# Softmax sums of two attention layers: pairs on VectorE, accumulating DMAs for the rest

## The chip, the cores and the metric

The kernel runs on one core of one Trainium2 chip. The metric is the device time of one execution in microseconds (us), lower is better. The three timed runs of the kernel before lie between 2926.52 and 2927.66 us, with a median of 2927.6 us.

## The reference, cut to what matters

The input is x of shape (4, 64, 64, 64): four images, each of 4096 tokens with 64 channels, all float32. Four attention layers follow each other. The change touches only layers 2 and 3, which have the same core once queries, keys and values are there:

```
# layer 2, per image (layer 3: the same with h for xn and other weights; it returns h + proj)
w   = jnp.einsum('bchw,bcHW->bhwHW', q, k) * scale     # 4096 x 4096 scores
w   = jax.nn.softmax(w.reshape(B, H, W, H * W), axis=-1)
out = jnp.einsum('bhwHW,bcHW->bchw', w, v)
out = linear_last(out, Wp, bp)
return out + residual
```

The softmax needs, for each of 4096 queries, the sum of 4096 exponentials. The kernel takes no maximum first; it computes exp(score) directly, multiplies it with the values, and divides by the sum at the end.

## The kernel before, in words

**Tiles.** An image lies in SBUF as [128, 2048]: 64 channels of one half of the tokens on partitions 0 to 63, of the other half on 64 to 127. `attention` (layers 2 and 3, from line 1272) walks over 4 chunks c of 1024 queries, and within a chunk over 32 blocks j of 128 keys. `first(u)` (u = 32 c + j) makes the scores of one key block on TensorE, four matmuls of 64x64 tiles into a PSUM tile `s` of 128 keys x 1024 queries (line 1288), and ScalarE turns them into a tile `p` of exponentials (line 1293). Only two `s` tiles exist, and `p` tiles come from a pool of 14 buffers. `then(u)` (line 1323) multiplies `p` with the values and accumulates in PSUM.

**Sums.** VectorE adds the 32 `p` tiles of a chunk into one tile `zacc`, element by element: 31 additions of 128x1024 (line 1299). The sum over the 128 keys of a block is left to `turn_blocks`: a transpose by blocks of 32 (line 1307), a reduction over 32 columns (`sum_blocks`, line 1311, giving `zsums`), and eight small matmuls on TensorE that add the rest (`sums`, line 1242). Then VectorE takes the reciprocal, and `turn` (line 1257) transposes and divides the output `o`.

**Order.** The schedule is written out by hand: the order of calls is the order of instructions on each engine. One `step` makes two key blocks: `first(2t)`, `first(2t+1)`, then the two `then` of two steps ago with a piece of background work between them (`advance(MID)`) and after or in the middle of the second (`advance(LATE)`), and last whatever was put on the list `later`. `before[n]` runs at the start of step n. `urgent` holds work with a due step. Background work is the preparation of other images and layer 1 of another image, one piece per `yield`. With t the last step of a chunk, the order before is: `turn_blocks` at the end of step t, `sum_blocks` at the end of step t+1, the last `then` of the chunk in step t+2 followed on ScalarE by a copy of half the output (line 1332) and on VectorE by adding the other half (line 1333), and `turn` with its `sums` matmuls in the middle of step t+4 (line 1334 puts it on `urgent`). There are 4 chunks x 2 layers x 4 images = 32 chunks. The very last one of the kernel is handled by `final` instead of `turn`.

**Queues.** Instructions of an engine start in order. SP issues nearly all DMAs. GpSimd (POOL) runs in this part only the power function in `inverse_root` (line 767), for the normalisations, and at the very end two stores.

## Time and profile before

| | us |
|---|---|
| median of the timed runs | 2927.6 |
| span of the profiled execution (first to last instruction; its time is not given apart from it) | 2927.0 |
| TensorE matmuls busy | 2895.3 (99%) |
| VectorE busy | 1871.5 (64%) |
| of it `zacc` additions of line 1299, 960 + 32 | 1174.2 + 38.9 |
| ScalarE busy | 1800.3 (62%) |
| GpSimd busy | 35.2 (1%) |
| DMA engines, mean busy share of queue q1 | 4.8% |

Busy time is the time in which an engine worked on at least one instruction. A busy TensorE need not run at its peak, since matmuls overlap, so the pace of a step is read from start to start. The mean granted clock of TensorE is 0.998 of full speed. In the profile's groups a row has the line, engine, operation, names and shapes, the count, the busy time, the mean of one in ns, and the idle time of the engine before it with what ended it.

### The profile page before, as it was taken

The page shows a single profiled execution, that of the slowest core. Times are in us where ns is not written, and L with a number is a line of the kernel's source. Part 1 is how long each engine was busy: PE and PEld are TensorE (multiplying, and loading weights), DVE is VectorE, ACT ScalarE, POOL GpSimd, SP SyncE. Part 2 cuts the span into 40 slices and gives each one's busy share as a digit, 9 for nine tenths or more (in the row PEclk, how much of TensorE's full clock was granted, in tenths as well). Part 3 has the DMA queues.
Part 4 walks back from the last instruction along what each step waited for, and adds up shares of the span by engine and source line. Part 5 has one row for each costly group of instructions (what it writes and reads, how often), then busy time and mean ns, then how long its engine had stood idle before and what let it go on. Part 6 is the DMA issues. An engine that isn't in the chain of part 4 may idle for free.

```text
span 2927.0 us, 66546 instructions
## 1 busy us (share of the span) xinstructions
PE 2895.3 (99%) x29397; PEld 1113.6 (38%) x29397; DVE 1871.5 (64%) x2141; ACT 1800.3 (62%) x2481; POOL 35.2 (1%) x35
## 2 busy tenths in 40 slices
PE   9999999999999999999999999999999999999998
PEld 3333233333444433344443343333344444443333
DVE  2111753589821078963027897888888877878878
ACT  5666666665566766566766655555555655555554
POOL 0000000000000000000000000000000000000000
PEclk9999999999999999999999999999999999999999
DMA  2010000000001000000000000000000000000000
GB/s 38 1 30 7 1 1 16 7 5 5 19 5 30 1 7 5 5 23 16 1 1 7 5 9 19 19 5 9 5 19 8 20 5 8 6 20 5 8 5 10
DMA packets 85513, 30.64 MB, mean 10 GB/s; under 512 B 79168, under 2 KB 83264, under 8 KB 83808
## 3 DMA queue, kind: packets, MB, share of 16 engines
q1 hardware_dynamic: 83168, 25.87, 4.8%
q8 instruction: 232, 3.80, 0.6%
q10 hardware_dynamic: 1984, 0.38, 0.1%
q14 instruction: 65, 0.53, 0.1%
q0 software_dynamic: 64, 0.07, 0.0%
HBM read 4.79 MB, written 4.19 MB: 3 GB/s over the span
## 4 chain that ended last, share of the span: by engine, by line
PE 97%; DVE 1%; ACT 1%; issue 0%; DMA 0%; POOL 0%; ACTq 0%; DVEq 0%
PE acc L1323 30%; PE s L1288 30%; PE s L999 15%; PE acc L1028 15%; PE s L1122 2%; PE acc L1148 2%; ACT p L1128 1%; DVE zacc L1299 1%; PE s L1148 1%; PE s L891 0%; PE s L912 0%; PE s L1419 0%; PE s L1467 0%; PE s L1092 0%; PE s L1194 0%
## 5 line engine op out<-in xcount | busy, mean ns | idle before, releaser
L1293 ACT ACTIVATE p<-s 128x1024 f32<-128x1024 f32 x1024 | 994.6, 1022 | 696.2 <-PE s L1288 676.5
L1299 DVE TENSOR_TENSOR zacc<-zacc,p 128x1024 f32<-128x1024 f32 x960 | 1174.2, 1223 | 179.7 <-ACT p L1293 114.8
L1323 PE MATMUL acc<-p,v 64*64 64x512 f32 (+1 forms) x8576 | 1006.6, 573 | 0.0
L1009 ACT ACTIVATE p<-s 128x1024 f32<-128x1024 f32 x480 | 487.3, 1020 | 114.8 <-PE s L999 114.6
L1323 PEld LDWEIGHTS acc<-p,v 64*64 64x64 f32 x8576 | 340.4, 133 | 545.1 <-issue 545.1
L1028 PE MATMUL acc<-p,vs 64*64 64x512 f32 (+1 forms) x4224 | 501.4, 577 | 0.0
L1288 PE MATMUL s<-q,k 64*64 64x512 f32 x2048 | 491.6, 590 | 2.1 <-ACT p L1128 2.1
L999 PE MATMUL s<-xT,q 64*64 64x512 f32 x2048 | 487.2, 591 | 2.4 <-DVE mean L1355 0.7
L1288 PE MATMUL s<-q,xT 64*64 64x512 f32 x2048 | 489.5, 591 | 0.0
L999 PE MATMUL s<-xT,q_swapped 64*64 64x512 f32 x2048 | 487.6, 591 | 0.3 <-DVE o L1157 0.3
L1288 PE MATMUL s<-q,h_swapped 64*64 64x512 f32 x2048 | 481.0, 591 | 3.9 <-DVE v L916 3.5
L1288 PE MATMUL s<-q,k_swapped 64*64 64x512 f32 x2048 | 480.4, 590 | 0.0
L1011 DVE TENSOR_REDUCE all_z<-z 128x1 f32<-128x4 f32 x128 | 20.1, 157 | 606.5 <-ACT p L1009 606.2
L1028 PEld LDWEIGHTS acc<-p,vs 64*64 64x64 f32 x4224 | 173.3, 133 | 266.0 <-issue 264.2
L1288 PEld LDWEIGHTS s<-q,h_swapped 64*64 64x64 f32 x2048 | 145.5, 133 | 144.5 <-issue 131.7
L1288 PEld LDWEIGHTS s<-q,k_swapped 64*64 64x64 f32 x2048 | 148.1, 133 | 137.6 <-issue 87.2
L999 PEld LDWEIGHTS s<-xT,q_swapped 64*64 64x64 f32 x2048 | 146.2, 133 | 141.8 <-issue 110.3
L1288 PEld LDWEIGHTS s<-q,xT 64*64 64x64 f32 x2048 | 145.7, 133 | 138.1 <-issue 131.7
L999 PEld LDWEIGHTS s<-xT,q 64*64 64x64 f32 x2048 | 144.2, 133 | 139.3 <-issue 110.8
L1288 PEld LDWEIGHTS s<-q,k 64*64 64x64 f32 x2048 | 148.6, 133 | 116.7 <-issue 96.2
L1017 ACT ACTIVATE vs<-v,all_r 128x64 f32<-128x64 f32 x256 | 89.1, 348 | 157.2 <-PE acc L1028 80.3
L1128 ACT ACTIVATE p<-s 128x1024 f32<-128x1024 f32 x128 | 124.1, 1022 | 82.4 <-PE s L1122 78.5
(213 smaller groups left out, 1319.6 us busy)
## 6 DMA issues: line engine op xcount, KB each, us to landing
k_swapped<-k SPq DMA_DIRECT2D x8, 512.0 KB, 5.8
residual<-turned SPq DMA_DIRECT2D x128, 32.0 KB, 1.9
h_swapped<-xT SPq DMA_DIRECT2D x8, 512.0 KB, 5.3
out_dram<-turned SPq DMA_DIRECT2D x60, 64.0 KB, 2.0
xin<-in_x_dram SPq DMA_DIRECT2D x12, 256.0 KB, 6.8
q_swapped<-q SPq DMA_DIRECT2D x6, 512.0 KB, 5.5
pg<-pg SPq DMA_DIRECT2D x8, 128.0 KB, 2.3
xin<-in_x_dram SPq DMA_DIRECT2D x12, 64.0 KB, 2.4
```

The lines of the kernel that those rows point to most:

```text
L999: nc.tensor.matmul(s[half(e), chunk(i)], queries(m, i, e), k[half(i), chunk(c)], start=True, stop=True)
L1009: nc.scalar.activation(p, s, AF.Exp, accum_out=z)
L1011: nc.vector.tensor_reduce(zsum[:, m : m + 1], zs.pop(m), AX.X, ALU.add)
L1017: nc.scalar.activation(vs, v[:, m, :], AF.Copy, scale=rz[:, m : m + 1])
L1028: nc.tensor.matmul(acc[c][half(i), cols], scaled[t][half(e), :], ps[NC * m + c][half(e), chunk(i)][:, cols], start=(m == 0 and not second) ...
L1122: nc.tensor.matmul(ss[e][half(m), chunk(i)], pgs[0 if e == d else 1][r, ds(n * P + m * C, C)], th[r, chunk(i ^ j)], start=True, stop=True,)
L1128: nc.scalar.activation(pk[e], ss[e], AF.Exp)
L1148: nc.tensor.matmul(acc[quarter(q), :], g[:, k, :], ps[j, k][q // 2][:, chunk(q % 2)], start=(k == 0 or not bank), stop=(k == NK - 1 or not ...
L1288: nc.tensor.matmul(s[half(e), chunk(i)], k[(j + i) % 2][half(i), ds(j // 2 * P + e * C, C)], q[half(i), chunk(c)], start=True, stop=True,)
L1293: nc.scalar.activation(p, s, AF.Exp)
L1299: add = lambda: nc.vector.tensor_tensor(zaccs[c], p0, p, ALU.add)
L1323: nc.tensor.matmul(accs[c][e][half(i), cols], v[half(e), j, :], p[half(e), chunk(i)][:, cols], start=(j == 0), stop=(j == NB - 1),)
```

## The change

VectorE no longer adds every `p` to `zacc`. In every step it adds the two new key blocks to each other. The first two pairs of a chunk (n = 0 and 1) are the two accumulators of the chunk; they lie in a pool of three `zacc` buffers instead of two. Each later pair (n = 2 to 15) goes to a tile of the `p` pool, and a DMA issued by GpSimd adds it into accumulator n % 2. The `p` pool has 13 buffers instead of 14. `turn_blocks` runs two steps later than before and first adds the two accumulators. In the last chunk of the kernel (`at_once`) VectorE adds the pairs itself and `turn_blocks` keeps its place.

```diff
-    x_p, p_p, z_p, o_p = pool("x", 13), pool("p", 14), pool("z", 2), pool("o", 2)
+    x_p, p_p, z_p, o_p = pool("x", 13), pool("p", 13), pool("z", 2), pool("o", 2)
@@ attention, first(u)
             p = ps[u] = p_tile()
             nc.scalar.activation(p, s, AF.Exp)
-            if j == 1:
-                zaccs[c] = z_p.tile([P, 1024], FP, tag="zacc", name="zacc")
-            if j >= 1:
-
-                p0 = ps[u - 1] if j == 1 else zaccs[c]
-                add = lambda: nc.vector.tensor_tensor(zaccs[c], p0, p, ALU.add)
-                later.append(add) if j % 2 or urgent_now() or ready(MID) else add()
+            if j % 2:
+                p0, n = ps[u - 1], j // 2
+                at_once = c == NC - 1 and final is not None
+                pair = p_tile() if n > 1 else z_p.tile([P, 1024], FP, tag="zacc", name="zacc", bufs=3)
+                if n < 2:
+                    zaccs[c, n] = pair
+
+                def add():
+                    nc.vector.tensor_tensor(pair, p0, p, ALU.add)
+                    if n > 1 and at_once:
+                        nc.vector.tensor_tensor(zaccs[c, n % 2], zaccs[c, n % 2], pair, ALU.add)
+                    elif n > 1:
+                        nc.gpsimd.dma_start(zaccs[c, n % 2], pair, accum_op=ALU.add)
+
+                later.append(add)
             if j == NB - 1:
-                later.append(lambda: turn_blocks(c))
+                if at_once:
+                    later.append(lambda: turn_blocks(c))
+                else:
+                    before.setdefault(now[0] + 2, []).append(lambda: later.append(lambda: turn_blocks(c)))
 
         def turn_blocks(c):
 
             t = p_tile()
-            nc.vector.transpose(t, zaccs.pop(c))
+            z = zaccs.pop((c, 0))
+            nc.vector.tensor_tensor(z, z, zaccs.pop((c, 1)), ALU.add)
+            nc.vector.transpose(t, z)
 
             def sum_blocks():
                 zsums[c] = small.tile([P, 32], FP, tag="zsums", name="zsums")
```

## The prediction

> **What bounds the kernel now.** I read the busy rows and slices, then the costliest groups, then short windows, then what VectorE does around the places that the change moves.

> ```profile
> span 2927.0 us, 66546 instructions
> PE 2895.3 (99%) x29397; PEld 1113.6 (38%) x29397; DVE 1871.5 (64%) x2141; ACT 1800.3 (62%) x2481; POOL 35.2 (1%) x35
> DVE  2111753589821078963027897888888877878878
> L1299 DVE TENSOR_TENSOR zacc<-zacc,p 128x1024 f32<-128x1024 f32 x960 | 1174.2, 1223 | 179.7 <-ACT p L1293 114.8
> ```

> TensorE is busy for all but 31.7 us. The next view is one step of two key blocks in layer 3 without background work (columns: stretch, length, then busy time and count of PE, PEld, DVE, ACT and POOL, granted clock, DMA share, GB/s):

> ```profile
> 2012.50:2015.93 3.43, 3.43 (x36) 1.20 (x32) 2.45 (x2) 1.94 (x2) 0.00 (x0) 1.00 0.02 5
> ```

> A step lasts 3.43 us at full clock, PE covers all of it, and VectorE needs 2.45, so in a plain step VectorE hides. Of the steps without background work, nearly all last 3.43; one in layers 2 and 3 stands out with 9.8 us, at 1784.8:

> ```profile
> 1783.26 1.23 DVE L916 TENSOR_TENSOR v<-s,bv 128x1024 f32<-128x1024 f32 x1 [3.33 <-PE s L912]
> 1784.40 2.54 DVE L1299 TENSOR_TENSOR zacc<-zacc,p 128x1024 f32<-128x1024 f32 x2
> 1786.98 1.25 DVE L1307 STREAM_TRANSPOSE p<-zacc 128x1024 f32<-128x1024 f32 x1
> 1788.15 1.19 DVE L916 TENSOR_TENSOR v<-s,bv 128x1024 f32<-128x1024 f32 x1
> 1789.39 1.12 PE L1288 MATMUL s<-q,h_swapped 64*64 64x512 f32 x2 [3.53 <-DVE v L916]
> ```

> There PE waits 3.53 us for a second L916 that stands behind two `zacc` additions and the transpose, and the windows show the clock at 0.50 from 1789.4 to 1795.3. Elsewhere VectorE is off the path. So the ceiling of a gain is small, and what matters is what becomes late.

> **The change part by part.** The programs as built have the same order of instructions on PE, ACT and SP; only VectorE and POOL differ.

> *Fewer additions.* 992 of 1.22 us become 512 pairs, 14 more in the last chunk, and 32 that join the two accumulators: 558, or 434 x 1.22 = 530 us less on VectorE. Hidden under PE in plain steps: 0. At 1784.8 only one pair (1.22) stands before the second L916 instead of 2.54 + 1.25, so it ends near 1786.75 and PE restarts near 1786.8 instead of 1789.39: 2.6 us. The idle gap is then about 1 us, for which I expect no clock loss, and half of 5.9 us, 2.95, comes back too. Gain 5.5 us; without the clock's part 2.6.

> *The later turn.* This is the part on the path. The view is a chunk boundary in layer 3, VectorE's rows, then one row of PE:

> ```profile
> 2017.33 1.25 DVE L1307 STREAM_TRANSPOSE p<-zacc 128x1024 f32<-128x1024 f32 x1
> 2018.61 1.22 DVE L1311 TENSOR_REDUCE zsums<-p 128x32 f32<-128x1024 f32 x1
> 2023.63 0.69 DVE L1333 TENSOR_TENSOR o<-o,acc 128x512 f32<-128x512 f32 x1 [1.55 <-ACT o L1332]
> 2024.24 5.14 DVE L1299 TENSOR_TENSOR zacc<-zacc,p 128x1024 f32<-128x1024 f32 x4
> ...
> 2028.81 0.25 PE L1242 MATMUL s<-zsums,lanes 64*64 64x16 f32 x8
> ```

> `zsums` is ready at 2019.83, 9 us before PE wants it. In the new order on VectorE the addition of the accumulators and the transpose stand behind L1333 (end 2024.32), then comes pair n = 1 of the next chunk, then the reduction. From the end of L1333: addition 1.22, transpose 1.25, pair 1.22, reduction 1.21, with the small gaps and overlaps of neighbours here 4.79, and 0.15 until PE starts (reduction end to matmul at the kernel's end: 2916.72 to 2916.87): 4.94 us. Before, 4.49 us lie between the end of L1333 and the matmul. PE is in order, so the second `then` and all that follows wait 0.45 us. PE is the bound, so it is lost.

> There are 31 such boundaries (the last chunk keeps its place). Asking the timeline at each for the end of L1333 and the start of L1242 gives 4.37 to 4.49 us at 23, 6.27 at 3, 5.14 at 2, 3.67 at 2, 5.48 at one. The built order shows what else stands before the reduction. 23 x 0.47 = 10.7. Of these, three (second chunk of layer 2 beside layer 1) have two operations of L1187/L1188 there, 0.68 + 0.71 each: +4.2; three have one in-place scaling of h (0.81, 0.81, 0.74): +2.3; one a tiny reduction: +0.2. The 6.27 ones have two layer-1 additions: 4.94 + 2.45 - 6.27 = 1.1 each, 3.4. The 5.14 ones: 0. The 3.67 ones have a tiny reduction (0.22) in place of the pair: 0.3 each, 0.5. The 5.48 one has two of L1424: 0.8. Sum 22.1 us.

> *The end.* In the last chunk the chain after the last exponential (2912.45) is pair, add to accumulator, join, transpose, reduce instead of the rest of two additions, transpose, reduce:

> ```profile
> 2911.56 2.55 DVE L1299 TENSOR_TENSOR zacc<-zacc,p 128x1024 f32<-128x1024 f32 x2 [0.88 <-ACT p L1293]
> 2914.22 1.25 DVE L1307 STREAM_TRANSPOSE p<-zacc 128x1024 f32<-128x1024 f32 x1
> ```

> Three additions from 2912.45 end near 2916.2 instead of 2914.11. PE already waits for `zsums` there: +1.9 us.

> *The DMAs.* 434 of 512 KB, one per 3.43 us. Before has none, so I bound one. Nearest rows:

> ```profile
> k_swapped<-k SPq DMA_DIRECT2D x8, 512.0 KB, 5.8
> residual<-turned SPq DMA_DIRECT2D x128, 32.0 KB, 1.9
> out_dram<-turned POOLq DMA_DIRECT2D x2, 32.0 KB, 3.0
> ```

> They may take long in two ways. The built program makes DMA n wait on POOL for DMA n-2 (same accumulator), so each must land within 2 x 3.43 = 6.87 us of its issue; and the join waits for DMA 15, issued about 4.5 us after the start of step t, while VectorE reaches the join 11.8 us after it: 7.3 us. `k_swapped` goes as two transfers, issued 0.5 us apart: 1 MB in about 6.3 us; less 1.9 fixed that is 2.2 us per 512 KB. [...] Below 0 there is nothing: no DMA replaces one on the path.

> *Buffers.* 13 `p` buffers also hold pairs. In the built program most pair buffers are written again three or four steps later (10 us or more), but 36, beside layer 1, are taken by an exponential two steps later. Steps there last 5.64 us, so 2 x 5.64 + 2.1 - 4.5 = 8.9 us for the DMA: 0 at 5.4 us. Past that ACT stalls, and with two `s` tiles PE follows.

> *POOL's own work.* `pow` for the normalisations (5.4 us at 128x32, 1.5 at 128x1) now shares its queue with waiting DMA issues. Of the layer-2 ones only one falls among the DMAs; it holds DMA issues by 5.4 us once, and the joins come steps later. 0 to 5, I take 0.

> Sum against the profiled execution: 2927.0 + 22.1 + 1.9 - 5.5 = 2945.5; the timed median lies 0.6 above that span, so 2946 us.

> **The rivals.** [...]

> *The turn is not late* (faster): if the boundary chain is under 4.5 us, say because the join can run before L1333, the 22 us vanish and the gain at 1784.8 stays: 2927.6 - 5.5 = 2922, or 2924 with the end's 1.9. The built order puts L1333 first, which speaks against it. It decides if the chain shrinks by 0.45 us.

> *No change*: part of the waits is absorbed and cancels the gain: 2927.6. PE's steps at exactly 3.43 us leave no slack for it.

> **How the numbers follow.** 0.58 for my case (2938 to 2956), 0.31 for late DMAs, 0.06 for no change, 0.05 for faster. 0.2% (5.9 us) is about what a measurement here can tell from none; the first two cases are slower by more: 0.89. The range leaves out the 0.11 below and the top quarter of late DMAs, 0.08: 2934 to 3110.

> **What would show it.** Right: PE idle of about 0.5 us before L1242 at most boundaries, ended by VectorE's reduction; accumulating DMAs landing in 5 to 6.5 us; no 0.50 clock at 1785; plain steps still 3.43; VectorE busy 530 us less. Wrong: long waits of POOL for DMAs or of the join for them, plain steps over 3.5, or ACT waiting for buffers.

## The result, and the profile after

The changed kernel takes 2956.31 us in the median of four runs (2954.01 to 2958.77) against 2927.11 (2926.52 to 2927.66) for the kernel before: 29.2 us more, a ratio of 1.0099 with a 95% interval of 1.0085 to 1.0113. It is slower, as forecast, and inside the range of 2934 to 3110, but 10 us above the predicted 2946 and at the upper edge of the prediction's own case (2938 to 2956).

The span of the profiled execution is 2952.3 us, and its own time is 2954.01, the shortest of the four. The distance between span and time is 1.7 to 2.1 us in every later run, so the profiled execution of the kernel before, with a span of 2927.0, took about 1.5 us more than its median, and the 0.6 us of the prediction was too small. The two spans therefore differ by 25.3 us only, where the medians differ by 29.2; the parts below are those of these two executions.

From the page of the kernel after: the busy rows and two of the rows of slices, the row of GpSimd's DMA queue (packets, MB, share of the 16 engines' span), then two of the costliest groups.

```profile
span 2952.3 us, 66631 instructions
PE 2899.5 (98%) x29397; PEld 1154.3 (39%) x29397; DVE 1342.7 (45%) x1707; ACT 1800.3 (61%) x2481; POOL 405.5 (14%) x469
...
DVE  2211752466530056642015665455555445545447
...
DMA  2010000546601055650015577768767776776871
...
q0 software_dynamic: 62560, 227.63, 41.1%
...
L1302 DVE TENSOR_TENSOR p<-p 128x1024 f32<-128x1024 f32 x448 | 547.7, 1223 | 530.7 <-ACT p L1293 517.4
L1306 POOL DMA_DIRECT2D zacc<-p x434 | 369.5, 851 | 1929.7 <-DVE p L1302 1280.3
```

VectorE is busy 529 us less (forecast 530), and outside the transition none of it is seen in the time. In layer 3 its slices fall from 8 to 5 tenths, and the DMA engines go from nearly nothing to 7 tenths. The DMAs' own rows on the same page:

```profile
zacc<-p POOLq DMA_DIRECT2D x434, 512.0 KB, 4.9
...
residual<-turned SPq DMA_DIRECT2D x128, 32.0 KB, 4.6
out_dram<-turned SPq DMA_DIRECT2D x60, 64.0 KB, 5.5
```

An accumulating DMA lands 4.9 us after its issue in the median, a little under the 5.4 us that the prediction counts with. But transfers of SP that run beside it need 4.6 us in place of 1.9 (`residual`), 5.5 in place of 2.0 (`out_dram`) and 8.2 in place of 5.3 (`h_swapped`).

At the transition (before: 3.53 us of waiting and half clock) the timeline shows, VectorE's rows and then TensorE's:

```profile
1797.03 1.23 DVE L916 TENSOR_TENSOR v<-s,bv 128x1024 f32<-128x1024 f32 x1 [3.74 <-PE s L912]
1798.17 1.22 DVE L1302 TENSOR_TENSOR p<-p 128x1024 f32<-128x1024 f32 x1
1799.30 1.22 DVE L916 TENSOR_TENSOR v<-s,bv 128x1024 f32<-128x1024 f32 x1
...
1800.58 0.65 PE L1288 MATMUL s<-q,h_swapped 64*64 64x512 f32 x2 [0.95 <-DVE v L916]
```

and the window over it (stretch, length, busy time of PE, PEld, DVE, ACT, POOL, clock, DMA share, GB/s):

```profile
1800.00:1802.00 2.00, 1.43 (x16) 0.60 (x20) 0.52 (x1) 0.92 (x2) 0.53 (x1) 1.00 0.88 166
```

One pair stands between the two L916, TensorE waits 0.95 us, and the clock stays at 1.00. Step by step, from start to start of TensorE's steps, the two steps here last 4.65 and 3.43 us where they lasted 9.78 and 3.79: 5.5 us gained, as forecast.

The chunk boundary that the prediction showed, in the kernel after:

```profile
2034.52 0.69 DVE L1346 TENSOR_TENSOR o<-o,acc 128x512 f32<-128x512 f32 x1 [2.27 <-ACT o L1345]
2035.12 1.22 DVE L1319 TENSOR_TENSOR zacc<-zacc 128x1024 f32<-128x1024 f32 x1
2036.38 1.25 DVE L1320 STREAM_TRANSPOSE p<-zacc 128x1024 f32<-128x1024 f32 x1
2037.55 1.18 DVE L1302 TENSOR_TENSOR zacc<-p 128x1024 f32<-128x1024 f32 x1
2038.65 1.21 DVE L1324 TENSOR_REDUCE zsums<-p 128x32 f32<-128x1024 f32 x1
...
2040.00 0.30 PE L1242 MATMUL s<-zsums,lanes 64*64 64x16 f32 x8
```

The order is the forecast one. From the end of L1346 (2035.21) to the matmul are 4.79 us, where 4.94 were forecast, and the step with the `sums` lasts 3.90 us where it lasted 3.55. TensorE's waits over the whole kernel (engine, line and what it waited for: us in total, times, longest):

```profile
PE s L1242 <- DVE zsums L1324: 10.5, 9, 2.6
...
PE s L999 <- DVE mean L1368: 3.8, 2, 1.9
...
PE s L1480 <- DMA residual<-turned: 3.1, 4, 1.3
```

The first two rows stood at 0.4 and 0.7 us before, and the third did not exist: a projection of layer 2 waits for the slowed 32 KB transfers. The view leaves out waits under 0.15 us. At a plain boundary, as the one above, TensorE's records leave only 0.12 us idle in front of the `sums` matmuls although the step is 0.35 us longer, so the cost of the boundaries has to be read from step to step and not from this row.

At the first of the two layer ends VectorE's rows are now:

```profile
806.15 1.22 DVE L1319 TENSOR_TENSOR zacc<-zacc 128x1024 f32<-128x1024 f32 x1
807.40 1.25 DVE L1320 STREAM_TRANSPOSE p<-zacc 128x1024 f32<-128x1024 f32 x1
808.57 0.18 DVE L1368 TENSOR_REDUCE mean<-s 128x32 f32<-128x64 f32 x1
```

The `mean` reduction stands behind join and transpose, and TensorE waits for it.

Compared step by step over all 768 steps, the difference is made up of these parts:

| part | forecast, us | in the traces, us |
|---|---|---|
| steps with the `sums` matmuls after a chunk | +22.1 | +18.9 |
| two layer ends, TensorE waits for `mean` | in the row above | +3.1 |
| half clock for 3.4 us at 1308.9 us, after one of these two waits | 0 | +1.7 |
| layer-2 projections that wait for `residual` | 0 | +5.5 |
| exponentials of layer 1 whose buffer a DMA still holds (steps at 619, 625, 1119, 1619 us) | 0 | +2.2 |
| the transition | -5.5 | -5.5 |
| the end | +1.9 | +2.2 |
| one step at 2894 us (+0.6), small stalls that are gone (-1.4), the start (+0.6) | 0 | -0.2 |

The parts come to 27.9 us, of 28.3 from the first step's start to TensorE's end. The spans differ by less because the first step of this execution starts 3.3 us earlier (at 9.87 us instead of 13.18); in the later runs it starts near 13 us.

### The profile page after: what moved, and what is told of

It is laid out like the page before. It is cut to its first block, busy times and chain, and to the rows that moved or that the text cites. A ratio compares the mean times of both kernels' runs of the same rounds, so it can differ in the third digit from the quotient of the medians.

```text
span 2952.3 us, 66631 instructions
## 1 busy us (share of the span) xinstructions
PE 2899.5 (98%) x29397; PEld 1154.3 (39%) x29397; DVE 1342.7 (45%) x1707; ACT 1800.3 (61%) x2481; POOL 405.5 (14%) x469
## 3 DMA queue, kind: packets, MB, share of 16 engines
q0 software_dynamic: 62560, 227.63, 41.1%
HBM read 4.79 MB, written 4.19 MB: 3 GB/s over the span
## 4 chain that ended last, share of the span: by engine, by line
PE 89%; issue 3%; DVE 3%; ACT 2%; DMA 1%; SPq 1%; POOL 0%; ACTq 0%; DVEq 0%; POOLq 0%
PE s L1288 27%; PE acc L1336 27%; PE s L999 15%; PE acc L1028 15%; PE s L1122 2%; PE acc L1148 1%; SPq L1471 1%; ACT p L1128 1%; DMA residual<-turned 1%; DVE p L1320 1%; PE s L1148 1%; DVE zacc L1319 1%; PE s L912 1%; DVE p L1302 0%; DMA zacc<-p 0%
## 5 line engine op out<-in xcount | busy, mean ns | idle before, releaser
L1293 ACT ACTIVATE p<-s 128x1024 f32<-128x1024 f32 x1024 | 995.4, 1022 | 713.8 <-PE s L1288 712.5
L1302 DVE TENSOR_TENSOR p<-p 128x1024 f32<-128x1024 f32 x448 | 547.7, 1223 | 530.7 <-ACT p L1293 517.4
L1306 POOL DMA_DIRECT2D zacc<-p x434 | 369.5, 851 | 1929.7 <-DVE p L1302 1280.3
L1336 PEld LDWEIGHTS acc<-p,v 64*64 64x64 f32 x8576 | 361.0, 133 | 524.5 <-issue 524.5
L1009 ACT ACTIVATE p<-s 128x1024 f32<-128x1024 f32 x480 | 486.9, 1020 | 119.2 <-PE s L999 119.0
L1288 PE MATMUL s<-q,k 64*64 64x512 f32 x2048 | 492.6, 590 | 3.1 <-ACT p L1128 3.1
L1288 PE MATMUL s<-q,xT 64*64 64x512 f32 x2048 | 493.1, 589 | 0.0
L1288 PE MATMUL s<-q,h_swapped 64*64 64x512 f32 x2048 | 479.5, 589 | 2.3 <-DVE k L1437 1.0
L1288 PE MATMUL s<-q,k_swapped 64*64 64x512 f32 x2048 | 480.3, 590 | 0.6 <-DVE mean L1368 0.6
L1288 PEld LDWEIGHTS s<-q,h_swapped 64*64 64x64 f32 x2048 | 154.8, 133 | 133.0 <-issue 120.6
L1288 PEld LDWEIGHTS s<-q,xT 64*64 64x64 f32 x2048 | 154.9, 133 | 127.3 <-issue 124.4
L1288 PEld LDWEIGHTS s<-q,k_swapped 64*64 64x64 f32 x2048 | 148.9, 133 | 137.4 <-issue 90.3
L1288 PEld LDWEIGHTS s<-q,k 64*64 64x64 f32 x2048 | 149.1, 133 | 115.7 <-issue 97.4
## 6 DMA issues: line engine op xcount, KB each, us to landing
zacc<-p POOLq DMA_DIRECT2D x434, 512.0 KB, 4.9
k_swapped<-k SPq DMA_DIRECT2D x8, 512.0 KB, 6.0
h_swapped<-xT SPq DMA_DIRECT2D x8, 512.0 KB, 8.2
q_swapped<-q SPq DMA_DIRECT2D x6, 512.0 KB, 5.5
```

The lines of the kernel that those rows point to most:

```text
L1009: nc.scalar.activation(p, s, AF.Exp, accum_out=z)
L1288: nc.tensor.matmul(s[half(e), chunk(i)], k[(j + i) % 2][half(i), ds(j // 2 * P + e * C, C)], q[half(i), chunk(c)], start=True, stop=True,)
L1293: nc.scalar.activation(p, s, AF.Exp)
L1302: nc.vector.tensor_tensor(pair, p0, p, ALU.add)
L1306: nc.gpsimd.dma_start(zaccs[c, n % 2], pair, accum_op=ALU.add)
L1336: nc.tensor.matmul(accs[c][e][half(i), cols], v[half(e), j, :], p[half(e), chunk(i)][:, cols], start=(j == 0), stop=(j == NB - 1),)
```

## The experiments

The theory: what is late on VectorE at the boundaries costs about 20 us, and the DMAs, though they keep up, cost 10 us through what shares the engines and the buffers with them. The rival: the DMAs make the lateness, so that without the late turn, or with a join placed earlier, the time would fall to that of the kernel before or below.

### What the DMAs cost

**13 buffers alone**, in the kernel before:

```diff
-    ... pool("p", 14), ...
+    ... pool("p", 13), ...
```

> The kernel before with 13 buffers of exponentials instead of 14, nothing else. Late turn and DMA theory: within 1 us of 2927. Buffer theory: a good part of the 29 us, 2935 us or more.

2927.01 us, ratio 0.9999 (0.9990 to 1.0007). The missing buffer costs nothing that can be told from none.

**Without the DMAs**, in the kernel after:

```diff
                     if n > 1 and at_once:
                         nc.vector.tensor_tensor(zaccs[c, n % 2], zaccs[c, n % 2], pair, ALU.add)
-                    elif n > 1:
-                        nc.gpsimd.dma_start(zaccs[c, n % 2], pair, accum_op=ALU.add)
```

> The accumulating DMAs are left out, so pairs 2 to 15 of 31 chunks are missing from the sums; the pair additions, their buffers, the late turn and the end stay. Late turn: the waits before the sums matmuls stay at about 20 us, and only the 5.5 us for late residual DMAs and about 2 us for buffers held by DMAs go: 2956 - 8 = about 2948 us, in 2944 to 2952. DMA theory: nearly all of the 29 us goes, below 2932 us. Buffer theory: the buffers are free earlier, so also most of it goes.

2946.18 us (ratio 1.0069, 1.0055 to 1.0083), so the DMAs cost 10.1 us of the 29.2, and the rest of the change 19.3. A row of its page, and two of TensorE's waits:

```profile
residual<-turned SPq DMA_DIRECT2D x128, 32.0 KB, 1.8
```

```profile
PE s L1242 <- DVE zsums L1322: 10.5, 9, 2.6
...
PE s L999 <- DVE mean L1366: 3.8, 2, 1.9
```

The small transfers are back at 1.8 us, no projection waits for them, and the waits for VectorE are the same to a tenth. So the lateness at the boundaries is VectorE's order alone. The step at 1308 us is not lengthened here: TensorE waits as long, but the clock stays up. The step at 2894 us is 0.6 us longer here too, so that is no cost of the DMAs.

**The layer-2 projection two steps later**, in the kernel after, so that the slowed transfers have time:

```diff
-                end = now[0] + (4 if spread is None else 6)
+                end = now[0] + (4 if spread is None else 8)
```

> The change with the output projection of layer 2 two steps later, so that its residual DMAs may take about 7 us longer. Theory that the accumulating DMAs delay these small DMAs and TensorE waits for them: the 4 to 5.5 us of waits before that projection go, 2951 to 2953 us. If those waits have another cause (VectorE late with the turn): no change, 2956 us.

2951.38 us (ratio 1.0084, 1.0070 to 1.0098), 4.9 us less than the kernel after. `residual` still takes 4.4 us to land, but TensorE's row of waiting for it is gone. So about half of the DMAs' 10 us is SP's small transfers being slow. Of the rest, 2.2 us are steps in which an exponential waits for a buffer until a DMA has landed; without the DMAs they are gone. The 1.7 us of half clock belong to that one execution. No run takes these apart, and 1 to 3 us of the 10 stay unexplained. The waits of the kernel after within 619 to 626 us show one of the buffers:

```profile
ACT p L1128 <- DMA zacc<-p: 2.0, 1, 2.0
```

### Where the turn may stand

**The join at the start of step t+2**, ahead of the addition of the outputs, in the kernel after:

```diff
-                    before.setdefault(now[0] + 2, []).append(lambda: later.append(lambda: turn_blocks(c)))
+                    before.setdefault(now[0] + 2, []).append(lambda: turn_blocks(c))
```

> Only the join of the two accumulators and the transpose move ahead of the last addition of the output on VectorE; every DMA, buffer and pair stays. Late turn (mine): the waits of TensorE before the sums matmuls (20.6 us in the profile of the change) and the 1.5 us waits behind the mean reduction at two layer ends shrink to below 3 us together, so 2956 - 21 = about 2935 us, in 2930 to 2941. DMA theory (the accumulating DMAs cost the time, by queue or by late landing): the join now waits for the last DMA, so no gain, 2950 us or more. Buffer theory: no change, 2954 to 2958 us.

2940.59 us (ratio 1.0045, 1.0031 to 1.0059), 15.7 us less than the kernel after, near the top of the expected range. The stall at a plain boundary is gone. In its place VectorE waits at the join:

```profile
DVE zacc L1319 <- DMA zacc<-p: 54.6, 28, 3.8
```

In the kernel after this row does not exist: by the time that the late join came, the last DMA had landed. Here 28 of 31 joins wait, 2 us in the mean. In plain steps VectorE has that time; where other work shares the step (both layer ends, and 2.0, 1.6 and 2.3 us in three steps of layer 3), it makes TensorE wait.

**The join in the last `then` of the chunk**, later than that and still ahead of the outputs:

```diff
                 if at_once:
                     later.append(lambda: turn_blocks(c))
-                else:
-                    before.setdefault(now[0] + 2, []).append(lambda: later.append(lambda: turn_blocks(c)))
...
                 acc = accs.pop(c)
+                turn_blocks(c)
                 nc.scalar.copy(o, acc[0])
```

> The change with the join and the transpose placed on VectorE just ahead of the output addition, inside the last then of the chunk, so behind the background work of that step and one and a half steps before the sums matmuls; DMAs and buffers stay. Late turn: the waits before the sums matmuls and behind the mean reduction (together 24 us) go, and unlike with the join at the start of the step VectorE no longer stands still for the last DMA: about 2933 us, in 2929 to 2937. If the accumulating DMAs land too late for any earlier join: about 2940 us, as with the join at the start of the step.

2941.4 us (ratio 1.005, 1.0036 to 1.0063): the second branch of the expectation by its number. The wait for the DMAs is smaller (33.8 us, 20 times), and the time is no better, so this wait is not all that is left.

**The same without the DMAs:**

> The kernel with the join in the last then of the chunk, ahead of the copy of o, with the accumulating DMAs left out (so pairs 2 to 15 of 31 chunks are missing from the sums; the rest of the work is the same). It tells what the remaining 14 us of that kernel are. If they are the DMAs (the join's wait for the last of them, the slower residual transfers), then only the end's 2.2, the transition's -5.5 and a few us are left: 2923 to 2928 us. If they are VectorE's order (join, transpose and reduction in front of the layer-end reductions whatever the DMAs do), 2936 to 2941.

2936.55 us (ratio 1.0032, 1.0020 to 1.0045). The first branch is missed: the DMAs are 4.9 us of what is left, and with none of them the kernel is still 9.7 us above the kernel before. This is where it is, at the end of layer 2 of the first image; VectorE's rows of this kernel, and TensorE's row last:

```profile
804.24 1.22 DVE L1315 TENSOR_TENSOR zacc<-zacc 128x1024 f32<-128x1024 f32 x1
805.50 1.25 DVE L1316 STREAM_TRANSPOSE p<-zacc 128x1024 f32<-128x1024 f32 x1
806.66 0.65 DVE L1343 TENSOR_TENSOR o<-o,acc 128x512 f32<-128x512 f32 x1
807.24 1.20 DVE L1320 TENSOR_REDUCE zsums<-p 128x32 f32<-128x1024 f32 x1
808.36 0.21 DVE L1365 TENSOR_REDUCE mean<-s 128x32 f32<-128x64 f32 x1
...
808.62 0.65 PE L999 MATMUL s<-xT,q 64*64 64x512 f32 x2 [3.00 <-DVE mean L1365]
```

and the same place before:

```profile
804.23 0.68 DVE L1333 TENSOR_TENSOR o<-o,acc 128x512 f32<-128x512 f32 x1
805.67 0.23 DVE L1355 TENSOR_REDUCE mean<-s 128x32 f32<-128x64 f32 x1 [0.77 <-PE s L1354]
...
805.95 0.65 PE L999 MATMUL s<-xT,q 64*64 64x512 f32 x2 [0.35 <-DVE mean L1355]
```

The `mean` reduction of 0.21 us is waited for by TensorE in both. Before, VectorE had been idle for 0.77 us when its operand came; here join, transpose, outputs and reduction stand in front of it. The two layer ends of this kind cost 4.4 us each in this execution: 2.7 of waiting, and 1.7 because the clock then falls to 0.50 for 3.4 us (from 809.2 and 1307.5 us). Two steps of layer 3 cost 2.0 and 0.7, the end 2.6. In the kernel after the join and the transpose stand there (the reduction comes behind), and the wait costs 1.5 at each. So VectorE has room over a whole chunk, but not at the places to which the turn has to move.

**That join, the later projection, and in the last chunk one addition for each key block as before** (its main lines; the third is for `at_once` alone):

```diff
+                turn_blocks(c)
                 nc.scalar.copy(o, acc[0])
...
-                end = now[0] + (4 if spread is None else 6)
+                end = now[0] + (4 if spread is None else 8)
...
+                one = lambda: nc.vector.tensor_tensor(zaccs[c, 0], q0, p, ALU.add)
```

> The former placement of the join, with the projection of layer 2 two steps later and the last chunk summed as before the change. What remains of the change's effects is the gain at 1785 (5.5 us), a few tenths elsewhere, and about 2 us of waits for buffers held by DMAs: 2923 to 2926 us, below the kernel before. If the DMAs cost TensorE in some other way, 2930 us or more.

2942.49 us (ratio 1.0046, 1.0032 to 1.0059): a miss by 17 us. Both mends do their work: the end is repaired (9.54 us from the start of the last step to TensorE's end, 9.45 before), and no projection waits for `residual`. But the joins still wait for DMAs (38.4 us, 21 times), each layer end costs 2.7 us, and several steps of layer 3 cost 1 to 3 us. Against the trace of the kernel with that join alone, 3.0 us more lost to half clock behind the layer ends and a step at 2603 us that is 2.9 us longer take back what the mends give. So this run does not tell what the two mends are worth.

**All pairs added by VectorE**, no DMA, and the turn at its old place:

```diff
-                at_once = c == NC - 1 and final is not None
+                at_once = True
```

> Every chunk is handled like the last one of the change: VectorE adds the pairs and adds them to the two accumulators, no DMA, and the turn keeps its place at the end of the chunk. VectorE does 31 additions a chunk as before, 13 buffers and pairs in the p pool stay. Late turn and DMA costs both gone: the gain at 1785 is gone too (more stands before the second values addition, about 1 us more idle) and the end costs 2 us: about 2931 us, in 2927 to 2936. Buffer theory (pairs in the p pool cost the time): 2945 us or more.

2927.95 us (ratio 1.0004, 0.9995 to 1.0012), no difference that can be told from none. VectorE makes as many additions as before (512 pairs, 448 into the accumulators, 32 joins: 992); the end costs 2.2, six other steps 0.45 to 0.77 each (3.4 together), and the transition gives 4.3, against expectation. There four operations (pair, accumulation, join, transpose) stand ahead of the second addition of `v`, but TensorE waits 1.13 us for an exponential and 0.78 for `v` where it waited once for 3.53, and the clock stays up; why the waits fall so is not shown. So the pairs alone cost about what the transition gives back, and what makes the kernel slower is the late turn and the DMAs.

### What gave the 5.5 us

**Every turn one step later in the kernel before**, except in the last chunk:

```diff
-                later.append(lambda: turn_blocks(c))
+                if c == NC - 1 and final is not None:
+                    later.append(lambda: turn_blocks(c))
+                else:
+                    before.setdefault(now[0] + 1, []).append(lambda: later.append(lambda: turn_blocks(c)))
```

> The kernel before with the transpose of the sums one step later (the reduction then comes behind the output addition, about 3 us ahead of TensorE's need), last chunk as before. Theory that the step of 9.8 us at 1784.8 is VectorE's queue plus a clock that falls after a long enough idle gap: the gap falls from 3.5 to about 2.3 us; 1.2 us are gained for certain, and 2.9 more if the clock stays up: 2926 or 2923 us. Theory that the late turn costs in itself wherever it is moved: slower than 2927 by some us.

2933.12 us (ratio 1.0021, 1.0013 to 1.0029), the last branch by its time: the transition gives 4.2 us as the first had it, and the later turns cost about 9 elsewhere (1.1 us in a step of layer 2 of each of three images, 0.6 to 1.1 in some others). With VectorE at its full load one step of delay is not free either.

**One turn alone later**, at the transition:

```diff
             if j == NB - 1:
-                later.append(lambda: turn_blocks(c))
+                if c == NC - 1 and name == "done2" and st["b"] == 2:
+                    before.setdefault(now[0] + 1, []).append(lambda: later.append(lambda: turn_blocks(c)))
+                else:
+                    later.append(lambda: turn_blocks(c))
```

> The kernel before, with the turn of one chunk alone (the last of layer 2 of image 2, the chunk at 1784.8 us) one step later, so that the second addition of v comes ahead of the transpose there. No pairs, no DMAs. If the gain at that transition needs nothing but the order of two VectorE instructions, it is what the kernel with every turn one step later showed there, 4.2 us (TensorE idle 2.3 us in place of 3.5 and no half clock), and nothing else moves: about 2923 us (2921.5 to 2924.5). If the clock falls there in spite of the shorter gap, about 2926. If the later reduction holds up the layer's end, 2927 or more.

2925.94 us (ratio 0.9996, 0.9988 to 1.0005): the branch in which the clock falls. The gap in this kernel's timeline, and a window behind it:

```profile
1787.86 0.85 PE L1288 MATMUL s<-q,h_swapped 64*64 64x512 f32 x2 [2.28 <-DVE v L916]
```

```profile
1789.00:1790.00 1.00, 1.00 (x8) 0.26 (x4) 0.00 (x0) 0.36 (x1) 0.00 (x0) 0.50 0.00 0
```

The same of the kernel with every turn one step later:

```profile
1792.96 0.65 PE L1288 MATMUL s<-q,h_swapped 64*64 64x512 f32 x2 [2.28 <-DVE v L916]
```

```profile
1793.00:1795.00 2.00, 2.00 (x20) 0.78 (x24) 1.06 (x1) 0.88 (x1) 0.00 (x0) 1.00 0.00 0
```

The same gap of 2.28 us, once with the fall and once without. The half clock lasts 3.4 us, to 1791.58, and takes 1.7 us of the gain.

**The same kernel once more:**

> The kernel with one turn alone moved one step later, profiled a second time, nothing changed. The gap at the transition must be 2.28 us again. If the gap alone decides, the clock falls to half for 3.4 us again and the run takes about 2926 us. If the phase of the clock's window against the program decides, it may as well stay at 1.00 as it did with every turn one step later at the same gap; then the run takes about 2924.3 us. A second fall leaves the two apart by nothing.

2925.89 us in a single execution, and the clock falls again for 3.4 us. By itself this leaves gap and phase undecided; the last section puts it beside the others.

**Additions and turn later at this one transition**, in the kernel before:

```diff
+                late = c == NC - 1 and name == "done2" and st["b"] == 2
+                if late and j >= NB - 2:
+                    before.setdefault(now[0] + 1, []).append(lambda: later.append(add))
+                else:
                     later.append(add) if j % 2 or urgent_now() or ready(MID) else add()
             if j == NB - 1:
+                if late:
+                    before.setdefault(now[0] + 1, []).append(lambda: later.append(lambda: turn_blocks(c)))
+                else:
                     later.append(lambda: turn_blocks(c))
```

> The kernel before, with the last two additions and the transpose of one chunk alone (the last of layer 2 of image 2, at 1784.8 us) one step later, so that both additions of v stand together ahead of them. If what the change gained at that transition is the order of VectorE there and nothing else, the gap falls to about 1 us, the step from 9.78 to about 4.7 us, the next from 3.79 to 3.43, and the clock stays up: 5.4 us less, 2921.5 us (2920.5 to 2923). With one turn moved alone a gap of 2.28 us was left and the clock still fell to half for 3.4 us; if a gap of 1 us can drop it too, about 2923.5. If the three operations moved behind hold up the next layer's start or the turn, 2925 or more.

2922.22 us (21 runs, 2920.61 to 2922.87) against 2927.18, ratio 0.9984 (0.9977 to 0.9990): faster than both kernels, by 5.0 us than the one before. VectorE's rows there, then TensorE's:

```profile
1782.93 1.23 DVE L916 TENSOR_TENSOR v<-s,bv 128x1024 f32<-128x1024 f32 x1 [3.33 <-PE s L912]
1784.73 1.23 DVE L916 TENSOR_TENSOR v<-s,bv 128x1024 f32<-128x1024 f32 x1 [0.57 <-PE s L912]
1785.87 2.55 DVE L1299 TENSOR_TENSOR zacc<-zacc,p 128x1024 f32<-128x1024 f32 x2
1788.45 1.25 DVE L1314 STREAM_TRANSPOSE p<-zacc 128x1024 f32<-128x1024 f32 x1
...
1786.01 0.65 PE L1288 MATMUL s<-q,h_swapped 64*64 64x512 f32 x2 [0.48 <-DVE v L916]
```

The gap is 0.48 us, the step lasts 4.17 us and the next 3.43, the clock stays up, and no other step differs from the kernel before by as much as 0.2 us. What the change gained is the order of three operations at one place; no DMA is needed for it.

## Why the prediction was right, and where its sum was off

*Direction and mechanism.* Right: the ceiling of the gain was the transition, and the later turn is on TensorE's path at the boundaries. With the DMAs left out the kernel takes 19.3 us more than the one before; the sum without them was 18.5.

*Fewer additions.* 529 us for 530, hidden; the transition 5.5 for 5.5 between the two profiled executions, with the clock up, as argued. Against other executions it is less: in the kernel before with 13 buffers the same gap brought 3.4 us of half clock and not 6.8, and the step lasted 8.93 us, so the gain would be 4.3.

*The later turn.* 18.9 and 3.1, 22.0 for 22.1, but by luck, from two errors that cancel. A plain boundary costs 0.35 us in place of 0.47, since the chain from the end of the outputs' addition to the matmul is 4.79 us and not 4.94: the neighbours on VectorE overlap by some 0.05 us more each. And the two boundaries of 3.67 us, put at 0.3 each ("a tiny reduction (0.22) in place of the pair"), cost 1.5. The step asked only what stands in front of the reduction of `zsums`. It did not ask what stands behind the join: `mean`, which TensorE waits for. That the clock would fall behind one of the two waits of 1.88 us there, to 0.50 for 3.4 us, which cost another 1.7, was not seen either.

*The end.* 2.2 for 1.9, where the prediction's own two times (2916.2 and 2914.11) would have given 2.1: pair, accumulation and join end at 2939.14, the matmul that waits for `zsums` starts at 2941.88.

*The DMAs.* This is the step that failed, in its size: the sum has nothing for them. No run shows where the 5.4 us of landing come from that the prediction counts with ("0 at 5.4 us"); the runs showed 4.9 us in the median. Its two limits held in the median, not throughout: 4.9 us is below 6.87 and 7.3, but 29 of the 434 took more than 6.87, up to 10.9. POOL waited for an earlier DMA 81 times, 212.3 us in all, which the prediction had named as a sign of being wrong, and VectorE waited for a pair's buffer four times, 11.7 us. None of this is seen in TensorE's steps: the late join never waits for a DMA, and plain steps last 3.43 us. Queue q0 is busy for 41.1% of 2952.3 us, 1213 us or 2.8 us for each of 434 DMAs: more than the 2.2 us for 512 KB that the prediction worked out from the row of `k_swapped`, and less than a step of 3.43 us. What was wrong is that only the DMAs' own landing was asked for. Nothing was asked of the transfers that share the 16 engines, although the prediction showed `residual` with its 1.9 us as a row. Measured: 10.1 us in place of 0, 4.9 of them gone with a later projection.

*Buffers.* 13 in place of 14 cost nothing. The forecast limit of 8.9 us for those beside layer 1 was too generous: four steps there became 0.5 to 0.6 us longer, with DMAs that land in 4.9 us in the median. In the three longest of these waits (2.0 us each) the DMA was not late: one was issued at 619.31 us, 0.3 us after its pair was done, and landed at 624.02. But the exponential had wanted the buffer 2.8 us after the issue, in the step after the pair's and not two steps later, so the step that failed is the count of steps behind the 8.9 us. The sign "ACT waiting for buffers" came here.

*POOL's own work.* 0 for 0: the kernels with and without the DMAs differ in no step by 0.2 us or more, apart from those named above and two at the start.

*The rivals.* No run shows a cost of late DMAs of the size that the 0.31 and the upper end of the range stand for: the late join waits for none of them, and the DMAs cost 10.1 us. A wait for the last of them took the place of the stall when the join was moved forward (28 waits). That the turn is not late is out; with the join moved forward, and even without DMAs, the kernel was 9.7 us slower than before.

## What to carry to other kernels

A moved step has to be priced for what stands behind it as well as for what stands in front of it, on its own engine and for every small result another engine waits for. A new stream of large DMAs that fits its own deadlines can still lengthen the small transfers beside it, here by 2.7 and 3.5 us, so look for those with less slack than that. When most of a change's gain sits at one place of the trace, try that place alone first: here reordering three operations once gave what a new way of summing could not.

## What the runs showed of the hardware

The 434 accumulating DMAs of 512 KB, between tiles of 128 partitions, landed in 4.9 us in the median (4.5 to 10.9), and their packets took 2.8 us of the 16 engines each; 32 KB and 64 KB transfers on SP's queue went from 1.9 and 2.0 us to 4.6 and 5.5 with them, and are at 1.8 and 2.0 with the DMAs left out.

The clock after a gap of TensorE did not follow the length of the gap alone. In one execution of the kernel after, the two layer ends have the same gap of 1.88 us; the first left the clock up, behind the second it was down for 3.4 us. TensorE's two rows in the timeline, and a window behind each:

```profile
808.81 0.65 PE L999 MATMUL s<-xT,q 64*64 64x512 f32 x2 [1.88 <-DVE mean L1368]
...
1307.63 0.65 PE L999 MATMUL s<-xT,q 64*64 64x512 f32 x2 [1.88 <-DVE mean L1368]
```

```profile
809.00:812.00 3.00, 3.00 (x39) 1.05 (x35) 0.90 (x1) 1.98 (x4) 0.00 (x0) 1.00 0.00 0
...
1309.00:1311.00 2.00, 2.00 (x16) 0.75 (x12) 0.00 (x0) 1.76 (x3) 0.00 (x0) 0.50 0.00 0
```

A gap of 3.53 us (before) brought 6.8 us of half clock, one of 3.54 (13 buffers) 3.4 us. After 2.28 us it was 3.4 us in both executions of one kernel and nothing in another; after 0.95 and 0.48 us nothing. In the two executions of the same kernel the fall came 0.3 us behind TensorE's restart (1788.17 against 1787.86) and 0.15 us ahead of it (1787.26 against 1787.41). So it is not a delay counted from the start of the gap.

```profile
807.11:810.52 3.41, 1.71 (x16) 0.67 (x20) 2.75 (x4) 1.19 (x4) 0.00 (x0) 1.00 0.00 0
1305.45:1308.87 3.42, 1.54 (x20) 0.70 (x24) 3.24 (x4) 1.19 (x4) 0.00 (x0) 1.00 0.02 5
...
1788.21:1791.62 3.41, 2.48 (x80) 1.27 (x72) 3.31 (x3) 0.88 (x1) 0.00 (x0) 1.00 0.02 5
1791.62:1795.03 3.41, 2.07 (x20) 0.82 (x24) 2.44 (x3) 1.06 (x2) 0.00 (x0) 1.00 0.00 0
...
1784.76:1788.17 3.41, 1.13 (x12) 0.21 (x8) 3.31 (x4) 1.02 (x1) 0.00 (x0) 1.00 0.00 0
```

Behind the windows in which TensorE is busy for 1.54 and 1.13 us the clock falls, behind those with 1.71, 2.48 and 2.07 it does not. Over all fourteen traces, from 20 us on, each of the 26 falls begins at the end of a window in which TensorE was idle for 55% or more, and no other window is idle for more than 56%. Ahead of the end, the fall also lasted a second window (6.8 us) in the two cases where TensorE filled the first to only 72% and 79%, and ended after one where it filled 86% or more.

For the reader of a profile: here a wait of 1.4 to 3.5 us cost another 1.5 to 1.7 us where enough idle time lay in one window of the grid, and 3.0 us where the fall lasted two windows (estimates: half of the time that TensorE ran at half clock). Where the windows lie changes from execution to execution, so one trace doesn't tell how often.
